# A second timetable for the units that run without row blocks, in a fused attention and state-space kernel

## The chip, the core and the metric

The kernel runs on one core of one Trainium2 chip. The metric is the device time of one execution in microseconds (us), as the median of three runs.

## The reference, cut to what matters

The input has 8 images of 256 channels and 48 x 48 = 2304 positions. Layer 0 is a top-16 attention between the positions of an image, layer 1 two stacked state-space (Mamba) blocks. Both add their result to their input:

```
x = x + L0(groupnorm(x))
    tokens @ W -> feat, pos;  pos /= |pos|;  sim = pos pos^T          (2304 x 2304)
    softmax over the 16 largest of each row, times feat
x = x + L1(groupnorm(x))          two times, d = 0 and 1:
    xn = layernorm(x);  xi, z = split(xn @ in_w);  xc = silu(conv4(xi))
    dt_r, B, C = split(xc @ xp_w);  dt = softplus(dt_r @ dtp_w + b)
    for t:  h = h * exp(dt[t] * A) + dt[t] * B[t] * x[t]              (512 channels x 16 states)
            y[t] = sum over states of h * C[t]
    x = ((y + xc * D) * silu(z)) @ out_w
```

## The kernel before

**Tiles and stages.** Positions are cut into 6 chunks of 384. One chunk of one block (c, d) is a *unit*; an image has 12 units, in an order in which block 1 follows block 0 by two chunks. A unit has 16 *steps* (32 of the 512 channels times 16 states, laid out as 128 partitions x 4 states), and a step has 2 *parts* of 2 states, so a unit is 32 parts and the program 8 x 12 x 32 = 3072 parts. The loop at the end of the kernel runs over the part number m. "Hook h" below is the place of a part within its unit, 0 to 31.

**What a part is.** ScalarE makes the decays exp(dt * A) into one of two PSUM banks (`decay`, L868, two instructions of 385 columns). VectorE runs the recurrence over them (`run_scan`, L883, 770 columns). The product with C is made either by VectorE directly after the scan (L885, 768 columns) or by GpSimd one step later (`pool_part`, L911, one instruction of 768 columns for one part of a step, or of 1536 for both). Who makes it is read from `SHARE`: three patterns of 16 letters, G for GpSimd and V for VectorE, read twice per unit. Pattern 0 is for units 1 to 9 of images that have a successor, pattern 1 for units 0, 10 and 11 of these, pattern 2 for the last image. GpSimd also makes the product dt * x * B, two steps ahead (`make_bx`, L844, 1536 columns a step), and dt * x (`times_x`, L792). TensorE sums over the states (`sum_states`, L929). On VectorE, `gate` (L935) takes that sum.

**The order of the work.** It is written out by hand in two tables, `between` (issued before the scan of a part) and `behind` (after it). A row `(7, copy_z, 0)` says that this function of unit w is issued at part 32 w + 7; places below 0 lie in the unit before, and places above 31 in the one after. Each engine works through its own instructions in this order. Around the change stand: the layer norm (`mean`, `center`, `square`, `variance`, `root`, `root_end`, `spread_root`, `scale`, `normal`; -37 to -22), the projections `in_proj` 0 to 7, `silu_x` (-14) and `softplus` (-10), which change ScalarE's table twice each, `times_x`, which also stores its results for the reload by `load_rep`, and `copy_z` / `silu_z`, which empty the projections 4 to 7 from PSUM. `out_proj` and `leave` of the unit before lie at hooks 6 to 8. The PSUM tiles of all of these, and of layer 0, come from one pool of three ("mm"). SyncE issues all transfers of the loop, in the same order; `load_rep` takes four for a step, into one of three dt buffers in turn.

**Layer 0 runs beside it.** Image 0's layer 0 runs alone at the start. For the other images a generator (`layer0`, stepped once a part by `Ahead.go`) makes one step after each scan: statistics of the input (6 chunks and 8 steps), then projections of the 6 chunks, then 18 row blocks, a new one every 16 parts. A row block has four VectorE instructions over 2304 columns. The generator of image 1 starts at part `EARLY` = -20; each next one starts as soon as its predecessor has ended. The row blocks begin only at a part that is in phase (`PHASE`, a multiple of 16). Before unit 0 of image b issues `load_v` (42 parts ahead of its first scan), `Ahead.finish` runs all steps that image b's generator has left, at once.

**Lines that the steps use.** L180 to L182 are the last three VectorE instructions of the reciprocal root (`rsqrt_end`); L164, L165 its start on ScalarE; L172 to L176 its end on GpSimd for layer 0's norms; L242 the input's statistics; L353, L357, L362 layer 0's copies on ScalarE; L530 the end of a row block; L676 `center`; L706 `scale`; L642 `in_proj`; L742 `taps`; L801 `copy_z`; L806 to L810 `silu_z`; L778 to L787 `softplus`; L960 `leave` of block 0; L616 `load_rep`.

Of the kernel before, what the change touches and what calls it, by code (L numbers as in the profile page):

```python
# [10 lines left out]
AF = mybir.ActivationFunctionType  # L11
# [4 lines left out]
P = 128  # L16
# [9 lines left out]
def tile_conv_preact(  # L26
# [44 lines left out]
    EARLY = -20  # L71


    SHARE = ("GGVGGGVVGGGGGGVG", "GGGVGVVGVVVGVGVG", "VGVGVGVVGGVVGGVG")
# [92 lines left out]
    def rsqrt_end(eng, r, var, eps, name):  # L167
# [11 lines left out]
        nc.scalar.activation(t, r, AF.Square)  # L179
        eng.scalar_tensor_tensor(var, var, eps, t, ALU.add, ALU.mult)  # L180
        eng.tensor_scalar(var, var, -0.5, 1.5, ALU.mult, ALU.add)
        eng.tensor_mul(r, var, r)  # L182
# [51 lines left out]
    def input_stats(b, pool, mm0, ahead, kept):  # L234
# [14 lines left out]
        found = []  # L249
        yield from group_stats(st, found, mm0, f"a{b}")  # L250
        known[b] = found

    def layer0(b, left, pool, ps0, alone):
# [27 lines left out]
        if not alone:  # L281
            if b not in known:
                yield from input_stats(b, pool, mm0, 2, None)
            loaded[0] = load_chunk(pool, x[b], 0, "x", f"xt_{b}_0", 3)
        yield
# [239 lines left out]
        def finish(t):  # L525
# [14 lines left out]
            (21, weights, 3), (4, top, 3), (14, turn, 0), (15, weights, 0), (6, others, 3),  # L540
            (-5, similar, 4), (-8, keep_similar, 0), (-5, keep_similar, 2), (24, turn_back), (18, weigh, 1),
            (17, weigh, 0), (1, top, 1), (-9, similar, 0), (-8, similar, 1), (-7, similar, 2),
            (22, average), (-6, similar, 3), (-7, keep_similar, 1), (-3, keep_similar, 3), (0, top, 0),
            (-3, keep_similar, 4), (15, turn, 1), (10, others, 4), (5, others, 0), (3, top, 2),
            (6, add_top), (11, invert), (5, others, 2), (17, turn, 2), (20, turn, 3),
            (15, weights, 1), (18, turn, 4), (18, weights, 2), (21, weigh, 3), (7, others, 1),
            (19, weigh, 2), (20, weights, 4), (21, weigh, 4), (24, finish),
# [126 lines left out]
    def center(unit):  # L674
        v = unit["v"]
        nc.vector.tensor_tensor(  # L676
            v, v, unit["lm"].unsqueeze(1).to_broadcast([P, CB, T]), ALU.subtract
        )
# [153 lines left out]
    def on_pool(unit, i, p):  # L832

        stage = 2 if unit["b"] + 1 == B else 0 if TOPK[0] <= unit["at"] < TOPK[1] else 1
        return SHARE[stage][(i * PARTS + p) % BLOCK] == "G"

# [115 lines left out]
    def leave(unit, cb):  # L952
# [18 lines left out]
        (-15, taps, 1), (38, out_proj, 0), (-15, taps, 2), (-14, taps, 3), (-34, square),  # L971
        (39, leave, 0), (23, load_rep, "dt", 14), (5, load_rep, "dt", 5), (-4, load_bc, 1), (38, out_proj, 1),
        (17, load_d, 2), (-17, tap, 1), (18, load_rep, "dtx", 13), (-8, times_x, 1), (19, gate, 1),
        (-22, normal), (1, load_rep, "dt", 3), (0, load_rep, "dtx", 4), (15, load_rep, "dt", 10), (6, load_rep, "dtx", 7),
        (10, load_rep, "dtx", 9), (12, load_rep, "dtx", 10), (20, load_rep, "dtx", 14), (11, gate, 0), (-29, spread_root),
        (-19, load_in, 5), (33, load_out), (-22, load_in, 0), (21, load_rep, "dt", 13), (-20, tap, 0),
        (-10, step_size, 1), (9, copy_z, 2), (-18, in_proj, 2), (2, load_rep, "dtx", 5), (10, sum_states, 0),
        (13, load_rep, "dt", 9), (29, gate, 2), (9, silu_z), (7, load_rep, "dt", 6), (19, load_rep, "dt", 12),
        (-6, load_rep, "dtx", 1), (-14, load_in, 7), (-30, root), (9, load_rep, "dt", 7), (4, load_d, 1),
        (-24, load_in, 3), (17, load_rep, "dt", 11), (14, load_rep, "dtx", 11), (-13, x_proj), (-17, load_in, 6),  # L980
        (-3, load_d, 0), (4, load_rep, "dtx", 6), (-4, load_rep, "dtx", 2), (-42, load_v),
    ]
    behind = [
        (-12, split), (-3, load_rep, "dt", 1), (3, in_proj, 4), (-10, step_size, 0), (-5, load_rep, "dt", 0),
        (-8, load_rep, "dtx", 0), (-15, tap, 3), (-1, load_rep, "dt", 2), (-28, scale), (16, load_rep, "dtx", 12),
        (11, load_rep, "dt", 8), (8, in_proj, 6), (17, sum_states, 1), (-14, silu_x), (25, load_rep, "dt", 15),
        (-37, affine), (1, times_x, 2), (7, copy_z, 0), (8, load_rep, "dtx", 8), (-17, tap, 2),
        (-10, softplus), (-16, in_proj, 3), (3, load_rep, "dt", 4), (-29, load_in, 2), (6, in_proj, 7),
        (35, gate, 3), (-2, load_rep, "dtx", 3), (8, copy_z, 1), (40, leave, 1), (-3, times_x, 3),
        (22, load_rep, "dtx", 15), (-16, load_in, 4), (29, load_d, 3), (-37, mean), (-19, taps, 0),  # L990
        (-19, in_proj, 1), (-10, load_bc, 0), (33, sum_states, 3), (-30, root_end), (-9, times_x, 0),
        (-22, load_in, 1),
    ]
    inner, outer = {}, {}
    for w, unit in enumerate(units):
        for table, rows in ((inner, between), (outer, behind)):
            for part, f, *args in rows:
                table.setdefault(HOOKS * w + part, []).append((f, unit, args))
# [91 lines left out]
```

## Time and profile before

| what | us |
|---|---|
| median of 3 runs (9910.5 to 9914.0) | 9911.15 |
| the profiled execution | 9912.53 |
| its span, first to last instruction | 9910.6 |
| layer 0 of image 0, up to the first scan | 463.0 |
| 12 units of image 0, from the first scan | 1214.5 |
| 12 units of image 2 | 1196.6 |
| 12 units of the last image | 1074.0 |
| VectorE / GpSimd / ScalarE / TensorE busy | 8963.6 / 8970.3 / 7319.0 / 7983.7 |

The profile gives for each engine the busy time and, for each idle stretch, what ended it. No engine is busy over the whole span, so the units are read one by one: the start of every 32nd scan cuts the span into units, and busy time, waits and order of instructions are read in these windows.

### The profile page before, as it was taken

Reading aid. Unit: us, or ns where it says so; the run is one execution under the profiler, and the core shown is the slowest. Engines: PE = TensorE matmul, PEld = TensorE weight load, DVE = VectorE, ACT = ScalarE, POOL = GpSimd, SP = SyncE. Lnnn points to the kernel's source line nnn. Section 1 sums busy time; section 2 is a strip of 40 time slices with the busy share of each in tenths; the row PEclk is TensorE's granted clock in tenths of the full one; section 3 lists DMA queues with packets and bytes.
Section 4 is the critical chain, followed back from the end, with each engine's and each line's share of the span. In section 5 each row is a group of like instructions: output and inputs, shape, how many; then the busy total and the mean of one; then the engine's idle time right before and its main releaser. Section 6 shows DMA issues by size and latency. Waiting matters only on the chain. (4 is left out here: it accounts for less than half of the span.)

```text
span 9910.6 us, 133908 instructions
## 1 busy us (share of the span) xinstructions
PE 7983.7 (81%) x36761; PEld 4396.4 (44%) x36761; DVE 8963.6 (90%) x7993; ACT 7319.0 (74%) x15966; POOL 8970.3 (91%) x3980
## 2 busy tenths in 40 slices
PE   8878887888878887788877888778887888866665
PEld 6634444444434454444444445344444444422222
DVE  5589997999989999899998999899998999988898
ACT  4577876777767777777777787777786777766766
POOL 1199997999989999899998999899998999999999
PEclk9989998899979998899988999889997999977777
DMA  1244444444444445444454444544445444544554
GB/s 35 58 124 131 129 134 131 133 125 136 129 140 128 132 130 145 129 126 134 131 145 126 130 130 133 142 130 123 137 129 147 121 134 126 139 136 132 144 139 122
DMA packets 1241871, 1269.01 MB, mean 128 GB/s; under 512 B 266496, under 2 KB 1214208, under 8 KB 1241120
## 3 DMA queue, kind: packets, MB, share of 16 engines
q1 hardware_dynamic: 1240576, 1260.46, 46.2%
q8 instruction: 293, 4.80, 0.2%
q14 instruction: 458, 3.75, 0.1%
q10 hardware_dynamic: 544, 0.00, 0.0%
HBM read 1046.58 MB, written 212.86 MB: 127 GB/s over the span
## 5 line engine op out<-in xcount | busy, mean ns | idle before, releaser
L844 POOL TENSOR_TENSOR bx<-BC,dtxr 128x1536 f32<-128x1536 f32 x1536 | 5298.3, 3452 | 168.6 <-PE y L929 114.9
L868 ACT ACTIVATE da<-dtr,A_sb 128x385 f32<-128x385 f32 x6144 | 3590.3, 585 | 880.8 <-DVE bx L883 540.0
L883 DVE TENSOR_TENSOR_SCAN bx<-da,bx 128x770 f32<-128x770 f32 x2040 | 3523.5, 1748 | 207.8 <-ACT da L868 166.0
L911 POOL TENSOR_TENSOR bx<-bx,BC 128x1536 f32<-128x1536 f32 (+1 forms) x1320 | 3303.7, 2503 | 246.2 <-DVE bx L883 232.0
L883 DVE TENSOR_TENSOR_SCAN da<-da,bx 128x770 f32<-128x770 f32 x1032 | 1809.9, 1754 | 212.4 <-ACT da L868 156.2
L642 PE MATMUL pe<-vn,inw 128*128 128x384 f32 (+1 forms) x3072 | 1248.8, 539 | 443.2 <-DVE xr L964 88.0
L433 PE MATMUL psim<-pos 128*128 128x512 f32 x2520 | 1225.5, 618 | 192.3 <-ACT sim L442 75.9
L504 PE MATMUL po<-feat,aT 128*128 128x256 f32 x5184 | 1359.6, 412 | 20.0 <-ACT aT L493 14.1
L929 PE MATMUL y<-bx,sel 128*32 128x384 f32 x12288 | 1234.1, 536 | 53.1 <-POOL bx L911 43.8
L504 PEld LDWEIGHTS po<-feat,aT 128*128 128x128 f32 x5184 | 1028.1, 205 | 356.4 <-issue 111.0
L885 DVE TENSOR_TENSOR bx<-da,BC 128x768 f32<-128x768 f32 x1032 | 989.3, 959 | 35.5
L642 PEld LDWEIGHTS pe<-vn,inw 128*128 128x128 f32 x3072 | 586.1, 205 | 950.9 <-issue 186.3
L433 PEld LDWEIGHTS psim<-pos 128*128 128x128 f32 x2520 | 486.6, 208 | 768.2 <-issue 414.0
L929 PEld LDWEIGHTS y<-bx,sel 128*32 128x32 f32 x12288 | 396.6, 119 | 879.2 <-issue 731.4
L742 DVE SCALAR_TENSOR_TENSOR xc<-pe,cw,xc 128x384 f32<-128x384 f32 x1152 | 696.6, 612 | 36.5 <-ACT xc L734 9.4
L772 PE MATMUL pd<-dbl,dtp_sb 16*128 16x384 f32 x768 | 437.1, 686 | 322.6 <-ACT dt L781 174.9
L899 ACT COPY h_st<-da 128x2 f32<-128x2 f32 x832 | 132.0, 159 | 687.7 <-DVE bx L885 681.1
L493 ACT ACTIVATE aT<-pt 128x512 f32<-128x512 f32 (+1 forms) x720 | 388.3, 548 | 244.3 <-PE pt L485 239.0
L484 PE MATMUL pt<-ident,sim 128*128 128x128 f32 x2592 | 536.2, 290 | 32.1 <-DVE v L706 16.0
L947 PE MATMUL pw<-z,ow 128*128 128x384 f32 x1536 | 525.1, 495 | 20.1 <-ACT h_st L899 7.3
L476 ACT ACTIVATE rest<-left,three 128x512 bf16<-128x512 f32 (+1 forms) x720 | 465.5, 670 | 52.3 <-DVE left L461 52.3
L485 PE MATMUL pt<-minus,rest 128*128 128x128 bf16 x2592 | 489.5, 224 | 5.9 <-ACT rest L476 5.8
(156 smaller groups left out, 9998.9 us busy)
## 6 DMA issues: line engine op xcount, KB each, us to landing
dtxr<-dtx_d SPq DMA_DIRECT2D x6144, 48.0 KB, 1.9
dtr<-dt_d SPq DMA_DIRECT2D x6144, 48.0 KB, 1.9
BC<-bc_d SPq DMA_DIRECT2D x768, 192.0 KB, 3.9
inw<-in_in_wT_dram SPq DMA_DIRECT2D x768, 128.0 KB, 2.3
dtx_d<-dtx SPq DMA_DIRECT2D x384, 192.0 KB, 2.1
dt_d<-dt SPq DMA_DIRECT2D x384, 192.0 KB, 2.3
ow<-in_out_wT_dram SPq DMA_DIRECT2D x96, 512.0 KB, 4.1
dmat<-diag SPq DMA_DIRECT2D x384, 64.0 KB, 2.3
```

The costliest lines, as they stand in the source:

```text
L433: nc.tensor.matmul(pm, pos[:, k, t * P : (t + 1) * P], pos[:, k, c0 : c0 + w], start=(k == 0), stop=(k == CB - 1),)
L484: nc.tensor.transpose(pt[:, q], row["sim"][:, r], ident)
L504: nc.tensor.matmul(row["po"], aT[:, m % PT, :], feat[:, m, :], start=(m == 0), stop=(m == NB - 1))
L642: nc.tensor.matmul(pe, w[:, k], unit["vn"][:, k, lo:], start=(k == 0), stop=(k == CB - 1))
L742: nc.vector.scalar_tensor_tensor(unit["xc"][e], unit["pe"][e][:, k : k + T], cw[:, unit["d"], e, k : k + 1], unit["xc"][e], ALU.mult, ALU.add,
L844: nc.gpsimd.tensor_tensor(bx[:, :, 1:], unit["BC"][0], unit["dtxr"][i].unsqueeze(1).to_broadcast([P, Q, T]), ALU.mult,)
L868: nc.scalar.activation(da[:, s * (1 + T) : (s + 1) * (1 + T)], unit["dtr"][i], AF.Exp, scale=A_sb[:, unit["d"], i, p * HQ + s : p * HQ + s ...
L883: nc.vector.tensor_tensor_scan(h, da, g, 0.0, ALU.mult, ALU.add)
L885: nc.vector.tensor_tensor(bx[:, :, 0:T], da.rearrange("p (q t) -> p q t", q=HQ)[:, :, 1:], unit["BC"][1][:, qs], ALU.mult,)
L911: nc.gpsimd.tensor_tensor(g[:, :, 0:T], g[:, :, 1:], unit["BC"][1][:, qs], ALU.mult)
L929: nc.tensor.matmul(y[j * G : (j + 1) * G, :], sel, unit["bx"][k * J + j][:, q, 0:T], start=False, stop=True, skip_group_check=True,)
L947: nc.tensor.matmul(pw, unit["ow"][:, k, cb * P : (cb + 1) * P], unit["z"][k], start=(k == 0), stop=(k == DB - 1),)
```

## The change

It has six parts.

1. `EARLY` becomes -24.
2. For images whose statistics are not known yet (2 to 7), `layer0` requests the first chunk before the group statistics and not after them, and has one step less.
3. `SHARE` has 32 letters a unit. Pattern 0 keeps 24 G and 8 V; patterns 1 and 2 go from 16 G to 17 G.
4. The Newton step on VectorE has two instructions in place of three: ScalarE's square is scaled by 1/2, and the result is negative. `center` therefore takes the mean minus the value.
5. In the timetable of the units beside row blocks, eight rows move.
6. A second pair of tables, `between_spare` and `behind_spare`, is used for all places outside units 1 to 9, and for the whole last image. 25 rows stand elsewhere than before, among them `copy_z` 0, `in_proj` 4 and 5, `taps` 0 and 1, `spread_root`, `scale`, `gate` 3, `times_x` 2 and 3, `load_bc` 0. In these tables `normal` (-22) is issued ahead of `scale` (-21), so it takes the value before that multiplication; and dt rows 14 are requested (20) into the buffer of rows 11 before the two decays of step 11 (issued at hooks 21 and 22), which then read rows 14. What these units compute differs in those two places.

```diff
-    EARLY = -20
-    SHARE = ("GGVGGGVVGGGGGGVG", "GGGVGVVGVVVGVGVG", "VGVGVGVVGGVVGGVG")
+    EARLY = -24
+    SHARE = (
+        "GGVGGGVVGGGGGGVGGGVVGGGVGGGGGGVG",
+        "GGGGVGVVGVVVGVGVGGGGVGVGGVVVGVGV",
+        "VGVGVGVGVGVGGGVGGGVVVGVVGGVVGGVG",
+    )
...
-        nc.scalar.activation(t, r, AF.Square)
+        nc.scalar.activation(t, r, AF.Square, scale=0.5 ** 0.5)
         eng.scalar_tensor_tensor(var, var, eps, t, ALU.add, ALU.mult)
-        eng.tensor_scalar(var, var, -0.5, 1.5, ALU.mult, ALU.add)
-        eng.tensor_mul(r, var, r)
+        eng.scalar_tensor_tensor(r, var, 1.5, r, ALU.subtract, ALU.mult)
...
+        if then is not None:
+            then()
         yield from group_stats(st, found, mm0, f"a{b}")
...
-            if b not in known:
-                yield from input_stats(b, pool, mm0, 2, None)
-            loaded[0] = load_chunk(pool, x[b], 0, "x", f"xt_{b}_0", 3)
-        yield
+            if b in known:
+                first_chunk()
+                yield
+            else:
+                yield from input_stats(b, pool, mm0, 2, None, first_chunk)
...
-            v, v, unit["lm"].unsqueeze(1).to_broadcast([P, CB, T]), ALU.subtract
+            v, unit["lm"].unsqueeze(1).to_broadcast([P, CB, T]), v, ALU.subtract
...
-        return SHARE[stage][(i * PARTS + p) % BLOCK] == "G"
+        return SHARE[stage][i * PARTS + p] == "G"
...
+    place = {(f, *args): part for part, f, *args in between + behind}
+
+    def beside_none(m):
+        image, part = divmod(m, HOOKS * len(order))
+        return image + 1 == B or not TOPK[0] * HOOKS <= part < TOPK[1] * HOOKS
```

Places that the text speaks of ("out" is behind the scan, "in" before it):

| row | before | beside row blocks | spare |
|---|---|---|---|
| load_rep dt 0 | -5 out | -3 out, after dt 1 | -5 out |
| times_x 3 | -3 out | 0 in | -8 out |
| load_in 4 | -16 out | -8 out | -16 out |
| load_rep dtx 8, 10, 14 | 8 out, 12 in, 20 in | 8 in, 10 out, 21 in | 9 in, 12 in, 20 in |
| load_rep dt 14 | 23 in | 23 in | 20 in |
| out_proj 0 | 38 in | 37 in | 38 in |
| copy_z 0 | 7 out | 7 out | 6 out |
| in_proj 4, 5 | 3 out, 7 in | the same | 4 out, 7 out |
| taps 1 | -15 in | -15 in | -15 out |
| spread_root, scale | -29 in, -28 out | the same | -22 in, -21 out |
| normal | -22 in | -22 in | -22 in |
| load_bc 0 | -10 out | -10 out | -12 out |
| mean, center | -37 out, -35 in | the same | -38 out, -34 in |
| gate 3 | 35 out | 35 out | 37 in |

## The prediction

> **What bounds the kernel now.** I read the page's busy times first. VectorE and GpSimd are both near nine tenths, so neither number alone says what a change is worth. Then I cut the span at every 32nd scan and asked for busy times by unit. Columns: start:end, length, then busy us of TensorE matmul, weight load, VectorE, ScalarE, GpSimd, then clock and DMA.
>
> ```profile
> PE 7983.7 (81%) x36761; PEld 4396.4 (44%) x36761; DVE 8963.6 (90%) x7993; ACT 7319.0 (74%) x15966; POOL 8970.3 (91%) x3980
> ...
> 1450.50:1570.50 120.00, 81.54 (x388) 45.99 (x386) 100.06 (x104) 75.20 (x173) 90.04 (x46) 0.81 0.48 135
> 2666.40:2768.70 102.30, 67.53 (x302) 33.74 (x300) 89.28 (x94) 67.73 (x157) 89.94 (x46) 0.77 0.56 157
> ...
> 4766.90:4863.80 96.90, 85.35 (x411) 48.11 (x410) 94.41 (x84) 77.66 (x173) 96.30 (x35) 0.94 0.47 129
> 5161.30:5268.40 107.10, 83.99 (x352) 46.25 (x351) 83.82 (x74) 76.73 (x161) 89.78 (x62) 0.85 0.48 134
> ...
> 8926.00:9015.60 89.60, 54.71 (x224) 24.35 (x223) 80.20 (x70) 63.33 (x145) 83.65 (x32) 0.77 0.49 136
> ```
>
> These are unit 10 of image 0, the same of image 1, unit 7 and unit 11 of image 3, and unit 1 of the last image. Beside row blocks (63 units, 95.6 to 101.7, mean 98.5) GpSimd is busy 96.3: nearly full. Units 10, 11 and 0 (21 units: medians 101.5, 107.2, 103.8) have less work and take longer; there it is waits. The last image (89.3) lies in between. So four places, four limits. The waits of each come next (engine, line, releaser: total, times, longest).
>
> ```profile
> DVE xr L530 <- PE pr L521: 11.2, 1, 11.2
> ...
> DVE da L883 <- ACT da L868: 9.4, 4, 6.9
> DVE z L935 <- PE y L929: 7.5, 3, 4.0
> DVE st L242 <- DMA xs<-in_x_dram: 6.2, 1, 6.2
> ...
> DVE da L883 <- ACT da L868: 31.2, 15, 3.2
> DVE bx L883 <- ACT da L868: 28.7, 16, 3.1
> ...
> L883 DVE TENSOR_TENSOR_SCAN bx<-da,bx 128x770 f32<-128x770 f32 x2040 | 3523.5, 1748 | 207.8 <-ACT da L868 166.0 <-POOL bx L856 32.8 <-POOL dtx L792 0.8
> ```
>
> The first row is unit 10 of image 0, the next three units 10 and 11 of image 3, then two of nine units of the last image. The last is the costliest group of scans over the whole run (count, busy, mean ns, then idle before them and by whom): 166.0 us until decays were there, 32.8 until GpSimd was. VectorE hardly waits for GpSimd: it waits for ScalarE's decays, behind table changes, and for TensorE.
>
> **A. Image 1's row blocks (EARLY).** Counting steps from the code: image 1's generator starts at -20, has its projections done at part 29, and the phase lets it begin only at 44. At 342 `finish` runs the 17 steps left at once: hook 21 of that unit lasts 16.1 us, of which VectorE waits 11.2 as shown. Starting at -24 it is done at 25 and begins at 28, as all later images do; one step is left at 342. Image 0 then costs what image 2 does: 1214.5 - 1196.6 = 17.9. Four steps move ahead of the first scan (two loads, two matmul groups of about 1.1); cost 0 to 4, taken 1. Sum -17, between -19 and -12.
>
> **B. The 63 units beside row blocks.** Pattern 0 moves one VectorE product from hook 22 to hook 19. At hook 20 VectorE waits 0.55 for decays (the mean), which the product then fills; at hook 22 it leaves 0.87 (start to start). The softplus burst behind hook 22 has its decays ready at 4744.1 in unit 6 of image 3, and the scan there starts at 4745.3, so it can come 0.9 earlier. The Newton step loses one instruction, 0.2 start to start (0.169 each in the rows). Together 1.07 less on VectorE. GpSimd has the same work, but of its 2.2 idle 1.5 are waits for a scan; that is all it can give back. Against it: dt 0 is requested two hooks later, behind dt 1. In that unit dt 1 is requested at 4760.2, 1.8 per four requests, so dt 0's last piece leaves at about 4763.4 and lands 1.9 later, 4765.3; its decay now starts at 4764.65, and the scan at 4767.0. Late by 0.7, of which 0.2 reaches the scan if it comes no earlier, more if it does. Behind this wait on ScalarE stand all decays. I take 1.0 - 0.4 = 0.6 a unit: 63 x 0.6 = -38. Bounds: 63 x 1.07 = -67, and +20 if the lateness eats it all and 0.3 more. `times_x` 3 moving to hook 0, its two stores past dt 0 and three requests of `load_rep`, `load_in` 4, dtx 8, 10, 14 and `out_proj` 0 move within stretches in which neither VectorE nor GpSimd waits above 0.1 a unit for a transfer; 0, and some tenths if that cover is gone.
>
> **C. Units 10, 11 and 0 of seven images.** VectorE loses one product (0.96) and one Newton instruction (0.2): 21 x 1.16 = -24. `copy_z` 0 one part earlier frees a PSUM tile. What that is worth shows in the last image: `in_proj` 7 (second row) stands 3.39 for a tile and runs when `leave` gives one; then ScalarE's second `copy_z` waits 1.74 for its matmul, and the scan 2.02.
>
> ```profile
> 8944.99 0.47 ACT L960 COPY vo<-pw 128x384 f32<-128x384 f32 x1
> 8945.52 5.60 PE L642 MATMUL pe<-vn,inw 128*128 128x384 f32 x12 [3.39 <-ACT vo L960]
> 8949.86 0.48 ACT L801 COPY z<-pe 128x384 f32<-128x384 f32 x1 [1.74 <-PE pe L642]
> 8951.55 1.77 DVE L883 TENSOR_TENSOR_SCAN da<-da,bx 128x770 f32<-128x770 f32 x1 [2.02 <-ACT da L868]
> ```
>
> In units 10, 11 and 0 the same place costs VectorE 4.0, 3.6 and 1.5 (gate for the sum); in unit 10 TensorE is then full of row-block matmuls, so not all of it goes. 0 to 2.7 each, taken 1.4: 20 x 1.4 = -28. One step less (part 2) moves layer 0's projections by one part: the start of the norm's root, two copies and a square (0.30 + 0.20 + 0.56 + 0.84 = 1.9) now come before and not behind the softplus of unit 11, where the scan waits 6.88 and GpSimd 4.17. ScalarE has 1.82 idle just ahead. 6 x 1.9 = -11, between 0 and -16; shifted elsewhere it may hit `silu_x`, up to +6. The first chunk's earlier request takes away ScalarE's 3.56 for it, but VectorE waits for GpSimd there (2.06): nothing. That wait is also where the added G costs: 1.685 a unit by the row of 768 columns, charged once per image, 7 x 1.7 = +12. `load_bc` 0 now stands directly behind the store that it reads (1.5 to land), ahead of the statistics' chunk: the 6.2 wait keeps or grows by 1.2; taken 0. Sum -51, between -100 and +10.
>
> Here a rule speaks against the change. The Trainium skill (GPSIMD Engine Reference, Engine selection) gives two-input elementwise work to VectorE because GpSimd is about twice as slow. By the rows it is 1.685 to 0.959, 1.76 times. By twice, the added products would cost 1.92, 33 x 0.23 = 8 more on GpSimd; still within its idle 11.8 to 18.4 a unit. So the move pays where VectorE is the later one, as here. For the bursts that stay, the same notes (ScalarE: Activation LUTs, What ACT_TABLE_LOAD costs) give 2.66 per change with a drain of 1.38. In the trace a load takes 1.283 and the first softplus starts 0.02 behind it. By the rule a burst would be 2.8 longer and the 1.9 would drown; by the row it counts.
>
> **D. The last image.** VectorE: 0.96 + 0.2 + the wait at hook 10 (mean 1.39) = 2.55 of 8.1 idle and 80.5 busy. GpSimd: 84.0 + 1.7 = 85.7, against 89.3 - 2.55 = 86.8; its waits for dt (1.45) and for the sum (0.6) may hold. I take 2.2: 12 x 2.2 = -26, between -36 and 0. `taps` 1 behind the scan moves a burst of 1.85; `spread_root`, `scale`, `gate` 3, mean and center keep their durations: 0. (For `center` the PSUM operand comes first now; `gate` has it first and takes 0.545 for 384 columns, the last addition of `leave` has it second and takes 0.539.)
>
> **The added wait.** In the spare units decays 11 read the buffer that dt 14 fills, requested at hook 20 and wanted at 21. Requests at hook 20 leave about one hook early and need 1.8 + 1.9. 0 to 1 each, taken 0.3: 33 x 0.3 = +10. Decays, scan and gate stand behind it.
>
> Sum: -17 - 38 - 51 - 26 + 10 = -122, from 9912.5 of the profiled execution (span 9910.6 and 1.9 around it). The median stands 1.4 lower: 9911.15 - 122 = 9789.
>
> **Rivals.**
> - *GpSimd is the bound* (0.22). B gives nothing, since 96.3 of 98.5 is full; C gives half (-25), D 1.0 a unit (-12), A stays: -17 - 25 - 12 + 10 = -44, 9867. For it: the busy row; against it: scans hardly wait for GpSimd.
> - *The waits of C dissolve* (0.15). Units 10, 11 and 0 fall to the 98.0 of their neighbours: 6 x (101.5 + 107.2 + 103.8 - 294) = -111 for -51, and B reaches -50: about -194, 9717. Against it: the statistics' wait and the bursts stay.
> - *Slower: dt 0 comes late* (0.05). BC pieces in that queue land up to 4.5 after request. If dt 0 does, decay 0 and all of ScalarE slip 2.6 in each of 63 units, +164 for -38: 164 - 17 - 51 - 26 + 10 = +80, 9991. It decides from 84 / 63 = 1.3 a unit. For it: it is asked behind dt 1 and BC; against it: SyncE is freed of two requests' waits.
> - *It doesn't do what it says* (0.03): the shift makes as many collisions as it removes, and VectorE's saving ends in ScalarE's waits: only A, and B to D cancel with the added wait: about 9900.
>
> **How the numbers follow.** My sum has 0.55. A measurement of this kernel can tell 0.2% (20 us) from no change. Faster: 0.55 + 0.22 + 0.15 = 0.92; same 0.03; slower 0.05. The range reaches from near the third case to the first rival with its spread: 9700 to 9878.
>
> **What would show it.** A: hook 21 of unit 10, image 0, falls from 16.1 to about 2. B: units 4 to 9 near 97.4, GpSimd's wait at hook 28 below 1. C: gate's wait at hook 10 smaller, the 6.88 near 5. D: `in_proj`'s 3.39 gone, units near 87. Wrong if decay 0 waits for dt 0, if the statistics' wait grows beyond 8, or if scans begin to wait for L844.

## The result, and the profile after

The changed kernel takes 9813.64 us (median of 4 runs, 9801.14 to 9814.34); the kernel before, measured again beside it, takes 9912.25. The ratio is 0.9898, with an interval of 0.988 to 0.9915. That is 99 us less; 122 were predicted. The profiled execution took 9813.77, its span 9812.0, which is 98.6 below the span before. The experiments are compared by the same two measures: the difference of the medians taken on the same chip, and the unit times of the profiled execution. The unit times come from one execution of each kernel. Some of their differences are scatter: `e1_early` and `e8_newton` change next to nothing in most units 11 and 0, yet the means of these units differ by up to about 1 between them and the kernel before. The first scan lies anywhere between 459.5 and 467.2. A single difference of that size says nothing.

The page's busy times come first, then two of its costliest groups (count, busy, mean ns, then idle before them and by whom).

```profile
span 9812.0 us, 133959 instructions
...
PE 7958.7 (81%) x36761; PEld 4336.7 (44%) x36761; DVE 8904.6 (91%) x7864; ACT 7304.4 (74%) x15938; POOL 9023.9 (92%) x3971
...
L892 DVE TENSOR_TENSOR_SCAN bx<-da,bx 128x770 f32<-128x770 f32 x2073 | 3578.1, 1747 | 263.6 <-ACT da L877 232.4
L920 POOL TENSOR_TENSOR bx<-bx,BC 128x1536 f32<-128x1536 f32 (+1 forms) x1311 | 3353.6, 2558 | 70.5 <-DVE bx L892 66.0
```

VectorE lost 59 us of work and GpSimd gained 54. The group of scans shown has those whose product GpSimd makes; it now waits 232.4 for decays, against 166.0 before. The other group has those whose product VectorE makes, before and after:

```profile
L883 DVE TENSOR_TENSOR_SCAN da<-da,bx 128x770 f32<-128x770 f32 x1032 | 1809.9, 1754 | 212.4 <-ACT da L868 156.2 <-POOL bx L856 20.5 <-POOL bx L844 15.8
```

```profile
L892 DVE TENSOR_TENSOR_SCAN da<-da,bx 128x770 f32<-128x770 f32 x999 | 1752.0, 1754 | 123.7 <-ACT da L877 81.2 <-POOL bx L865 15.6 <-ACT h_st L930 11.2
```

Together the scans wait 314 for decays where they waited 322. So VectorE has less work, but it waits for ScalarE almost as long as before. In two kernels that come below, `e10_four` and `e11_old_rows`, the same sum is 260 and 258. The scan is L892 now, the gate L944, the decay L877, GpSimd's product L920; `times_x` L801 and L804, `load_rep` L625, `in_proj` L651.

These are the units of the prediction's first block (columns as there): unit 10 of image 0, then unit 7, 10 and 11 of image 3, unit 0 of image 4, unit 1 of the last image.

```profile
1444.30:1547.80 103.50, 70.00 (x306) 34.50 (x304) 88.02 (x90) 67.16 (x154) 94.04 (x47) 0.76 0.58 159
4712.50:4810.80 98.30, 87.23 (x413) 48.43 (x412) 94.36 (x83) 77.80 (x175) 96.78 (x35) 0.93 0.48 130
5007.20:5113.50 106.30, 70.92 (x310) 35.63 (x312) 88.22 (x91) 67.27 (x155) 93.78 (x47) 0.76 0.55 157
5113.50:5214.60 101.10, 80.61 (x359) 44.80 (x360) 81.90 (x73) 78.64 (x162) 89.23 (x59) 0.91 0.52 141
5214.60:5311.00 96.40, 74.05 (x318) 37.76 (x318) 83.82 (x75) 70.62 (x152) 85.44 (x61) 0.84 0.46 123
8844.60:8931.00 86.40, 55.26 (x222) 23.54 (x222) 78.84 (x69) 63.16 (x144) 86.28 (x35) 0.80 0.52 141
```

Unit 10 of image 0 fell from 120.0 to 103.5, unit 11 of image 3 from 107.1 to 101.1. The unit beside row blocks, unit 7 of image 3, did not fall (96.9 to 98.3), and an ordinary unit 10 grew: 106.3, where 101.6 was the median of images 1 to 5. VectorE's waits in unit 10 and in unit 11 of image 3 and in nine units of the last image (total, times, longest):

```profile
DVE st L245 <- DMA xs<-in_x_dram: 7.3, 2, 5.9
DVE z L944 <- PE y L938: 4.8, 2, 4.2
DVE xr L973 <- PE pw L956: 2.4, 1, 2.4
DVE bx L892 <- ACT da L877: 2.2, 1, 2.2
DVE da L892 <- ACT da L877: 1.3, 1, 1.3
...
DVE bx L892 <- ACT da L877: 7.4, 2, 6.6
...
DVE bx L892 <- ACT da L877: 34.4, 23, 3.1
DVE z L944 <- PE y L938: 13.8, 7, 3.0
```

The burst's 11.2 is gone, but `gate` in unit 10 still waits 4.2 for the sum, and three waits (the third to fifth row) have joined it. In unit 11 the long wait for decays is 6.6 where it was 6.9. Both would have been clearly smaller had the prediction's part C been right in its parts.

Mean unit times of the profiled executions. "Beside" are units 1 to 9 of images 0 to 6 (63 units); 10, 11 and 0 are these units of images 0 to 6; 12 are of the last image.

| kernel | beside | unit 10 | unit 11 | unit 0 | last image | span |
|---|---|---|---|---|---|---|
| before | 98.26 | 103.27 | 104.62 | 103.98 | 89.50 | 9910.6 |
| after | 97.97 | 104.99 | 100.91 | 97.35 | 87.99 | 9812.0 |
| e1_early | 98.30 | 100.77 | 103.54 | 103.28 | 89.49 | 9884.9 |
| e2_chunk | 98.24 | 103.88 | 100.55 | 103.93 | 89.32 | 9881.7 |
| e3_share | 97.39 | 104.89 | 103.82 | 102.19 | 89.12 | 9843.9 |
| e4_copyz | 98.29 | 103.21 | 103.11 | 104.60 | 88.69 | 9895.2 |
| e8_newton | 98.20 | 103.60 | 104.23 | 104.11 | 89.49 | 9906.7 |
| e5_dt0 | 97.82 | 105.50 | 101.88 | 97.03 | 87.87 | 9808.9 |
| e6_u10 | 97.83 | 105.89 | 100.53 | 97.00 | 88.03 | 9810.5 |
| e9_dt14 | 97.93 | 104.02 | 98.10 | 98.95 | 89.49 | 9814.7 |
| e7_order | 97.87 | 103.56 | 98.09 | 101.25 | 89.36 | 9822.8 |
| e11_old_rows | 97.38 | 106.59 | 100.59 | 97.44 | 88.04 | 9784.5 |
| e10_four | 97.41 | 101.55 | 98.42 | 101.06 | 87.75 | 9759.6 |
| e12_mix | 97.41 | 103.63 | 97.99 | 101.26 | 87.76 | 9770.0 |

The account of the whole change, from the first two rows: first scan 1.9 earlier (within its scatter); beside row blocks 63 x -0.29 = -18.2; unit 10 of image 0 -16.4, of the six other images +4.7 each = +28.4; unit 11 -25.9; unit 0 -46.4; last image -18.2. Sum -98.6.

### The profile page after: what moved, and what is told of

Same layout as the page of the kernel before. It is cut to its first block, busy times and chain, and to the rows that moved or that the text cites. A ratio compares the mean times of both kernels' runs of the same rounds, so it can differ in the third digit from the quotient of the medians.

```text
span 9812.0 us, 133959 instructions
## 1 busy us (share of the span) xinstructions
PE 7958.7 (81%) x36761; PEld 4336.7 (44%) x36761; DVE 8904.6 (91%) x7864; ACT 7304.4 (74%) x15938; POOL 9023.9 (92%) x3971
## 4 chain that ended last, share of the span: by engine, by line
DVE 33%; ACT 24%; DMA 11%; PE 11%; SPq 10%; issue 7%; POOL 4%; ACTq 0%; DVEq 0%; POOLq 0%
DVE bx L892 11%; ACT da L877 10%; SPq L625 8%; DVE da L892 8%; DVE xc L751 5%; DMA dtr<-dt_d 4%; DVE bx L894 3%; DMA BC<-bc_d 3%; DVE top L464 2%; DVE left L467 2%; POOL bx L920 2%; PE po L514 2%; POOL bx L853 2%; DMA dtxr<-dtx_d 2%; ACT rest L486 1%
## 5 line engine op out<-in xcount | busy, mean ns | idle before, releaser
L877 ACT ACTIVATE da<-dtr,A_sb 128x385 f32<-128x385 f32 x6144 | 3588.1, 584 | 868.6 <-DVE bx L892 375.1
L892 DVE TENSOR_TENSOR_SCAN bx<-da,bx 128x770 f32<-128x770 f32 x2073 | 3578.1, 1747 | 263.6 <-ACT da L877 232.4
L920 POOL TENSOR_TENSOR bx<-bx,BC 128x1536 f32<-128x1536 f32 (+1 forms) x1311 | 3353.6, 2558 | 70.5 <-DVE bx L892 66.0
L892 DVE TENSOR_TENSOR_SCAN da<-da,bx 128x770 f32<-128x770 f32 x999 | 1752.0, 1754 | 123.7 <-ACT da L877 81.2
L651 PE MATMUL pe<-vn,inw 128*128 128x384 f32 (+1 forms) x3072 | 1214.7, 526 | 329.6 <-issue 50.9
L938 PE MATMUL y<-bx,sel 128*32 128x384 f32 x12288 | 1266.0, 536 | 109.9 <-POOL bx L920 103.1
L514 PEld LDWEIGHTS po<-feat,aT 128*128 128x128 f32 x5184 | 1022.4, 203 | 343.1 <-issue 107.2
L894 DVE TENSOR_TENSOR bx<-da,BC 128x768 f32<-128x768 f32 x999 | 957.2, 958 | 34.4
L651 PEld LDWEIGHTS pe<-vn,inw 128*128 128x128 f32 x3072 | 566.9, 199 | 845.8 <-issue 206.2
L956 PE MATMUL pw<-z,ow 128*128 128x384 f32 x1536 | 557.0, 509 | 112.8 <-ACT aT L503 52.4
L935 PE MATMUL y<-xc,dmat 128*128 128x384 f32 x768 | 398.3, 606 | 171.7 <-ACT h_st L930 58.5
```

The lines of the kernel that those rows point to most:

```text
L514: nc.tensor.matmul(row["po"], aT[:, m % PT, :], feat[:, m, :], start=(m == 0), stop=(m == NB - 1))
L651: nc.tensor.matmul(pe, w[:, k], unit["vn"][:, k, lo:], start=(k == 0), stop=(k == CB - 1))
L877: nc.scalar.activation(da[:, s * (1 + T) : (s + 1) * (1 + T)], unit["dtr"][i], AF.Exp, scale=A_sb[:, unit["d"], i, p * HQ + s : p * HQ + s ...
L892: nc.vector.tensor_tensor_scan(h, da, g, 0.0, ALU.mult, ALU.add)
L894: nc.vector.tensor_tensor(bx[:, :, 0:T], da.rearrange("p (q t) -> p q t", q=HQ)[:, :, 1:], unit["BC"][1][:, qs], ALU.mult,)
L920: nc.gpsimd.tensor_tensor(g[:, :, 0:T], g[:, :, 1:], unit["BC"][1][:, qs], ALU.mult)
```

## The experiments

My theory was the prediction's list: each part is worth its own term, and two terms cost (dt 0 late, the wait for dt 14). The rivals were that the second timetable brings the gain of units 10, 11 and 0, and that some other moved row eats what the patterns give. First each part by itself, on the kernel before; then parts undone in the changed one; then the parts that gained, put together.

The list of the change leaves out one row. In the row blocks' own timetable, `others` 3 (ScalarE makes 512 columns, 0.71) goes from part 6 of a block to part 7. The changed kernel and all kernels made from it have it at 7, the kernel before and all made from that at 6, and no run moves it alone. Beside row blocks it leaves no mark: `e11_old_rows` and `e12_mix` with it at 7 stand at 97.38 and 97.41, `e3_share` and `e10_four` with it at 6 at 97.39 and 97.41. Its last instance in image 3 lies at hook 29 of unit 9.

**Image 1's generator earlier.** `e1_early`:

```diff
-    EARLY = -20
+    EARLY = -24
```

> The kernel before with EARLY = -24 alone. Theory (step A): image 1's row blocks begin at part 28 and leave one step for the forced finish, so hook 21 of unit 10 of image 0 falls from 16.1 to about 2 and image 0 from 1214.5 to about 1197; time 9912 - 17 = 9895. Rival: the 17 forced steps cost what they cost anywhere, and come back as longer units 1 to 9 of image 0; time 9905 to 9912. The span up to the first scan should stay at 463 within 4 either way.

9890.72 against 9912.72, ratio 0.998 (0.9973 to 0.9987): -22. Unit 10 of image 0 fell from 120.0 to 102.3 and image 0 from 1214.5 to 1190.8 (1197 was worked out); the first scan came 2.0 later, which is within its scatter. Hook 21 of that unit lasts 2.7 here and 1.7 in the changed kernel, where it lasted 16.1. A stands as it was worked out; the rival, that the forced steps come back elsewhere, falls.

**The chunk ahead of the statistics.** `e2_chunk` is part 2 of the change, on the kernel before:

```diff
-            if b not in known:
-                yield from input_stats(b, pool, mm0, 2, None)
-            loaded[0] = load_chunk(pool, x[b], 0, "x", f"xt_{b}_0", 3)
-        yield
+            if b in known:
+                first_chunk()
+                yield
+            else:
+                yield from input_stats(b, pool, mm0, 2, None, first_chunk)
```

> The kernel before with the first chunk requested ahead of the group statistics, and so one step less, alone. In the changed kernel units 11 and 0 are 5 and 6.6 shorter, unit 10 is 4.7 longer. Theory 1: the shift by one part makes the gain of units 11 and 0 (fewer collisions of layer 0's ScalarE work with the table changes): units 11 and 0 fall by 3 or more each here, unit 10 stays; time 9912 - 6 x 8 = about 9865. Theory 2: the spare tables make it; here only the root's start in unit 11 (-1.9) counts: 6 x 1.9 = 11, time about 9900. GpSimd's 4.17 at hook 23 of unit 11 goes in either.

9881.75, ratio 0.9971 (0.9964 to 0.9977): -31, nearly three times the 11 of the prediction. Nearly all of it is unit 11: 4.1 at the mean of the seven, and 4.9 at the mean of the six beside which such a generator runs (107.2 to 102.3); units 0 and 10 keep their time within 0.7. GpSimd's wait of 4.2 for the root is gone there; in unit 11 of image 3 the scan's longest wait for ScalarE is 6.0 where it was 6.9. So unit 11 is as theory 1 has it and unit 0 as theory 2 has it, and the time lies between theirs.

**The patterns.** `e3_share` has the three patterns of 32 letters and nothing else:

```diff
-    SHARE = ("GGVGGGVVGGGGGGVG", "GGGVGVVGVVVGVGVG", "VGVGVGVVGGVVGGVG")
+    SHARE = (
+        "GGVGGGVVGGGGGGVGGGVVGGGVGGGGGGVG",
+        "GGGGVGVVGVVVGVGVGGGGVGVGGVVVGVGV",
+        "VGVGVGVGVGVGGGVGGGVVVGVVGGVVGGVG",
+    )
```

> The kernel before with the three new patterns of 32 letters alone. Theory (VectorE is the later one): units 1 to 9 lose 0.3 to 0.6 each, GpSimd's wait at hook 28 falls from 1.3 to below 0.3, the last image loses about 1.0 a unit, units 10, 11 and 0 about 1: -20 - 12 - 20 = time about 9860. Rival (GpSimd is the bound): units 1 to 9 move by less than 0.1, the last image does not gain from the added G and units 10, 11, 0 get longer by up to 1.7: time 9910 to 9945.

9845.18, ratio 0.994 (0.9925 to 0.9955): -67, of which 63 x 0.87 = 55 beside row blocks. This refutes the rival that GpSimd is the bound there. GpSimd's waits in units 1 to 9 of image 3, before and with the patterns:

```profile
POOL bx L911 <- DVE bx L883: 12.7, 15, 1.7
```

```profile
POOL bx L915 <- DVE bx L887: 1.4, 4, 0.5
```

It had 18.3 idle in these nine units (864.7 busy of 883.0), 12.7 of it waiting for a scan. 11.3 of that wait went, because VectorE's product now lies where VectorE waited (hook 20, 0.55 a unit, now 0). Part came back as other waits: 10.5 idle are left (866.0 busy of 876.5), and the nine units are 6.5 shorter.

**The copy one part earlier.** `e4_copyz`, in all units:

```diff
-        (-37, affine), (1, times_x, 2), (7, copy_z, 0), (8, load_rep, "dtx", 8), (-17, tap, 2),
+        (-37, affine), (1, times_x, 2), (6, copy_z, 0), (8, load_rep, "dtx", 8), (-17, tap, 2),
```

> The kernel before with copy_z 0 at 6 instead of 7 alone, in all units. Theory: the TensorE wait of 3.39 ahead of in_proj 7 shortens, the scan's wait for decays at hook 10 of the last image (mean 1.39) goes, units of the last image lose 1.4 (-17), units 10, 11 and 0 up to 1.4 (-28), the others nothing: time about 9870. Rival: the wait only changes its name (gate waits for the sum at hook 10, as the changed kernel's last image shows with 1.54): the last image moves by less than 0.3 a unit, time 9905 to 9912.

9901.22, ratio 0.9991 (0.9983 to 1.0): -11, at the edge of what can be told from nothing. The last image gains 0.81 a unit, between the theory's 1.4 and the rival's 0.3; units 10, 11 and 0 change by -0.06, -1.5 and +0.6, the others by 0. ScalarE's wait of the second copy, in nine units of the last image, before and in this kernel:

```profile
ACT z L801 <- PE pe L642: 13.1, 11, 2.9
```

```profile
ACT z L801 <- PE pe L642: 3.5, 9, 0.9
```

The mechanism is that of the prediction. In units 10, 11 and 0 it was carried over from the last image by likeness, and there it gives nothing that can be told from scatter.

**The shorter Newton step**, with `center` turned, `e8_newton`:

```diff
-        eng.tensor_scalar(var, var, -0.5, 1.5, ALU.mult, ALU.add)
-        eng.tensor_mul(r, var, r)
+        eng.scalar_tensor_tensor(r, var, 1.5, r, ALU.subtract, ALU.mult)
```

> The kernel before with the shorter Newton step and the turned center alone. Theory: 0.2 of VectorE's time a unit where VectorE is the later engine, and no other price for the operand order: 96 x 0.1 to 0.2 = 10 to 19 shorter, time 9893 to 9903. Rival: the saved instruction ends in the next wait for decays: within 5 of 9912. center should keep 0.947 within 0.01.

9909.34 against 9910.07, ratio 0.9995 (0.9987 to 1.0004). No difference that this measurement can tell, and a gain of more than 13 is excluded; 98.20 for 98.26 beside row blocks. `center` keeps its duration (0.945 after).

**dt 0 asked at its old place** in the changed kernel, `e5_dt0`. Here and in `e6_u10` and `e11_old_rows` the spare units keep the two places where the change computes something else; in `e9_dt14` the scaling alone does.

```diff
-        (-12, split), (-3, load_rep, "dt", 1), (3, in_proj, 4), (-10, step_size, 0), (-3, load_rep, "dt", 0),
+        (-12, split), (-3, load_rep, "dt", 1), (3, in_proj, 4), (-10, step_size, 0), (-5, load_rep, "dt", 0),
```

> The changed kernel with load_rep dt 0 back at -5 beside row blocks. Units 1 to 9 gained 0.87 each from the patterns alone and only 0.29 in the whole change. Theory: dt 0 behind dt 1 at -3 holds decay 0 and takes most of the difference, as the new waits of scans for decays at hooks 0 (0.48) and 6 (0.41) say: they go here, units 1 to 9 fall from 97.97 to about 97.4, time 9813 - 63 x 0.55 = about 9778. Rival: other rows of that table (times_x 3 at hook 0, load_in 4) make it: less than 0.15 a unit, time above 9803.

9808.19, ratio 0.9895 (0.988 to 0.991). Against the changed kernel's 0.9898 that is no difference; the unit times show 0.15 a unit beside row blocks (97.97 to 97.82), where the theory had 0.55. ScalarE's waits for dt in units 1 to 9 of image 3, in the changed kernel and in this one:

```profile
ACT da L877 <- DMA dtr<-dt_d: 29.5, 16, 3.7
```

```profile
ACT da L877 <- DMA dtr<-dt_d: 11.8, 7, 3.0
```

Sorted by place, over all 63 units, decay 0 (issued at hook 31) waits 1.94 a unit in the changed kernel and 0 here. So dt 0 does come late. But 11.8 remain, nearly all for decays at hook 5 (0.95 a unit over the 63). That is step 3, whose request nobody moved.

**Unit 10 on the other timetable.** `e6_u10`:

```diff
-        return image + 1 == B or not TOPK[0] * HOOKS <= part < TOPK[1] * HOOKS
+        return image + 1 == B or not TOPK[0] * HOOKS <= part < (TOPK[1] + 1) * HOOKS
```

> The changed kernel with the spare tables for units 0 and 11 and the last image only, unit 10 by the table beside row blocks. Unit 10 grew by 4.7 in the whole change and by nothing like it in the parts alone. Theory: the spare rows in unit 10 make it, where the last row blocks still fill TensorE until hook 12 (the addition of leave waits 1.67 for its matmuls at hook 6): unit 10 falls by 3 to 4.5, time 9813 - 7 x 3.5 = about 9790. Rival: the change of tables itself costs, and moves to unit 11, which grows by as much: within 5 of 9813.

9808.48, ratio 0.9896 (0.9881 to 0.9911). Unit 10 stays where it was: 107.2 as the median of images 1 to 5, against 106.2. The theory falls, and the rival's shift into unit 11 did not come either. So it isn't the spare table by itself that lengthens unit 10; with either of the new tables it is long, with the rows of before it is not (102.7 in `e10_four`).

The traces show what goes with it. In the changed kernel ScalarE's decays wait 2.8 for dt in the mean unit 10, nearly all at hooks 3 and 5; in all kernels with a new table there it is 2.5 to 4.6, and in the kernel before, `e3_share` and `e10_four` at most 0.1. Against `e10_four`, a unit 10 of the changed kernel is 3.44 longer, and hooks 5 and 6 together are 3.41 longer; the other hooks cancel. Step 3's decays in unit 10 of image 3, changed kernel and `e10_four`:

```profile
5019.10 1.20 ACT L877 ACTIVATE da<-dtr,A_sb 128x385 f32<-128x385 f32 x2 [1.49 <-DMA dtr<-dt_d]
```

```profile
4990.32 1.21 ACT L879 ACTIVATE da<-dtr,A_sb 128x385 f32<-128x385 f32 x2 [0.23 <-DMA dtr<-dt_d]
```

SyncE's queue at the start of that unit of the changed kernel, whose first scan is at 5007.2:

```profile
5008.04 0.34 SPq L804 DMA_DIRECT2D dtx_d<-dtx  x1
5008.43 0.42 SPq L804 DMA_DIRECT2D dt_d<-dt  x1
5008.94 1.79 SPq L625 DMA_DIRECT2D dtr<-dt_d  x4
```

The spare table has `times_x` 2 at hook -1, ahead of the request of dt 2, and the old one behind the request of dt 3. SyncE stands from 5006.61 until GpSimd's product, begun at 5007.01, is done, and dt 2 and dt 3 are requested 1.7 and 6.5 behind the first scan (0.8 and 5.8 in `e10_four`). In `e6_u10` it is `times_x` 3 at hook 0 that stands ahead of dt 3. No run moves these rows alone in unit 10, so this is read from the traces and not measured apart. Nor is it all: the waits do not put the kernels in the order of their unit 10 (`e12_mix` waits 3.6 at 103.63, the changed kernel 2.8 at 104.99).

**dt 14 back to hook 23** in the spare units, `e9_dt14`; and with it `spread_root` and `scale` back to their old places ahead of `normal`, `e7_order`:

```diff
-        (-15, taps, 2), (-14, taps, 3), (-35, square), (39, leave, 0), (20, load_rep, "dt", 14),
+        (-15, taps, 2), (-14, taps, 3), (-35, square), (39, leave, 0), (23, load_rep, "dt", 14),
```

```diff
-        (11, gate, 0), (-1, times_x, 2), (-22, spread_root), (-19, load_in, 5), (33, load_out),
+        (11, gate, 0), (-1, times_x, 2), (-29, spread_root), (-19, load_in, 5), (33, load_out),
...
-        (-8, times_x, 3), (-8, load_rep, "dtx", 0), (-15, tap, 3), (-1, load_rep, "dt", 2), (-21, scale),
+        (-8, times_x, 3), (-8, load_rep, "dtx", 0), (-15, tap, 3), (-1, load_rep, "dt", 2), (-28, scale),
```

> The changed kernel with dt 14 back at 23 in the spare tables, nothing else (normal still takes the value ahead of scale; the decays of step 11 read their own rows). With all three rows back, units 0 grew by 3.9 and the last image by 1.4 a unit, units 11 fell by 2.8. Theory: scale and spread_root made that (out_proj waits for the tile that scale frees), so here units 0 and the last image stay within 0.5: time 9808 to 9820. Rival: the later dt request makes it (SyncE then stands at hook 23 ahead of the stores of times_x): the last image grows by 1 or more a unit, time 9825 to 9845.

> The changed kernel with three spare rows back at the places before: spread_root -29, scale -28 (so normal again takes the scaled value) and dt 14 at 23 (so the decays of step 11 read their own rows). Units 0 lost 6.6 in the whole change and at most 1.8 in any part alone. Theory: the time does not hang on these rows; units 0, 11 and the last image stay within 0.5 each: time 9805 to 9825. Rival: the gain of unit 0 comes from taking the multiplication and its spread off hooks 3 and 4, where layer 0's projections and the out projection queue for the same three PSUM tiles: unit 0 grows by 3 to 6 again and the last image by 0.5 each: time 9840 to 9865.

`e9_dt14`: 9811.91, ratio 0.9896 (0.9878 to 0.9913), as the changed kernel within the interval. That hides movements in both directions. Unit 11 falls by 2.8 and unit 10 by 1.0; the last image rises by 1.5 a unit and unit 0 by 1.6. So the rival is right in the last image, though the time is the theory's. GpSimd's waits in nine units of the last image, changed kernel and `e9_dt14`:

```profile
POOL dtx L801 <- ACT dt L790: 9.4, 8, 1.5
POOL bx L920 <- DVE bx L892: 4.5, 5, 1.6
...
POOL dtx L801 <- DMA dtx_d<-dtx: 0.7, 1, 0.7
```

```profile
POOL dtx L801 <- DMA dtx_d<-dtx: 12.7, 8, 3.1
POOL dtx L801 <- ACT dt L790: 11.5, 9, 1.5
POOL bx L920 <- DVE bx L892: 4.5, 6, 1.6
```

With dt 14 asked at 23, GpSimd's next `times_x` waits 1.4 a unit for the store of an earlier one. In `e9_dt14` the requests of dt 14 stand ahead of that store, here in unit 3 of the last image:

```profile
9077.87 2.18 SPq L625 DMA_DIRECT2D dtr<-dt_d  x4
9080.15 0.37 SPq L804 DMA_DIRECT2D dtx_d<-dtx  x1
...
9082.25 1.00 POOL L801 TENSOR_TENSOR dtx<-dt,xc 128x384 f32<-128x384 f32 x1 [1.59 <-DMA dtx_d<-dtx]
```

GpSimd has little slack in these units (770.7 busy of 786.3 in the changed kernel), so this counts nearly in full: the nine units are 13.3 longer. But the wait is of the spare table's own making. That table has three `times_x` within two hooks (-9, -8, -8), the old one only two. In `e12_mix` the last image runs by the old table with dt 14 at 23: the wait is 0 there, and the unit takes 87.76. `e7_order`: 9824.95, ratio 0.991 (0.9895 to 0.9925); its span is 8 longer than that of `e9_dt14`, and unit 0 rises by another 2.3. Its theory, that units 0, 11 and the last image stay within 0.5, falls in all three. Of the 6.6 that unit 0 gained, about 2.3 came with the scaling behind `normal` and 1.6 with the early dt 14: 3.9 with the two places where the change computes something else.

**The eight rows beside row blocks put back.** `e11_old_rows` has `between` and `behind` as before the change, the rest as changed (only the eight rows are written out):

```diff
     between
-    (37, out_proj, 0), (0, times_x, 3), (8, load_rep, "dtx", 8), (21, load_rep, "dtx", 14),
+    (38, out_proj, 0), (12, load_rep, "dtx", 10), (20, load_rep, "dtx", 14),
     behind
-    (-3, load_rep, "dt", 0), (10, load_rep, "dtx", 10), (-8, load_in, 4), (-20, load_in, 1),
+    (-5, load_rep, "dt", 0), (8, load_rep, "dtx", 8), (-3, times_x, 3), (-16, load_in, 4), (-22, load_in, 1),
```

> The changed kernel with the rows beside row blocks all as before the change (the spare tables stay). Units 1 to 9 were 97.4 with the patterns alone and are 98.0 in the whole change; dt 0 back alone made 97.8. Theory: the eight moved rows together cost that: units 1 to 9 at 97.4, time 9813 - 63 x 0.55 = about 9778. Rival: the shorter Newton step or the state in which unit 0 hands over makes it: units 1 to 9 stay above 97.8, time above 9800.

9782.64 against 9917.75, ratio 0.9864 (0.9849 to 0.9879), as the theory has it, and a span 27.5 shorter than the changed kernel's. Beside row blocks a unit takes 97.38, as with the patterns alone (97.39). So the eight rows cost 0.59 a unit, 63 x 0.59 = 37, of which unit 10 gives some back. Nine units of image 3, changed kernel, this one, and the patterns alone (columns as in the blocks of units):

```profile
4123.10:5007.20 884.10, 766.72 (x3619) 422.97 (x3621) 850.27 (x740) 692.52 (x1520) 867.66 (x325) 0.93 0.49 131
```

```profile
4112.70:4990.40 877.70, 765.25 (x3610) 425.97 (x3609) 849.51 (x741) 693.95 (x1519) 866.31 (x323) 0.93 0.49 132
```

```profile
4143.20:5019.70 876.50, 760.85 (x3609) 425.89 (x3608) 850.69 (x750) 695.30 (x1519) 865.96 (x323) 0.93 0.48 132
```

All three have the same work on VectorE within 1.2 and on GpSimd within 1.7. The 6.4 between the first two are almost all waits. Which row makes them can be read from SyncE's queue at the start of unit 7 of image 3, whose first scan is at 4712.5 (changed kernel; start, duration, what is requested):

```profile
4714.04 1.76 SPq L625 DMA_DIRECT2D dtxr<-dtx_d  x4
4718.17 0.34 SPq L804 DMA_DIRECT2D dtx_d<-dtx  x1
4718.55 0.43 SPq L804 DMA_DIRECT2D dt_d<-dt  x1
4719.09 0.38 SPq L949 DMA_DIRECT2D ow<-in_out_wT_dram  x1
4719.57 1.90 SPq L625 DMA_DIRECT2D dtr<-dt_d  x4
```

and in the kernel before, first scan at 4767.0:

```profile
4767.73 1.75 SPq L616 DMA_DIRECT2D dtxr<-dtx_d  x4
4769.58 0.40 SPq L940 DMA_DIRECT2D ow<-in_out_wT_dram  x1
4770.08 1.84 SPq L616 DMA_DIRECT2D dtr<-dt_d  x4
4773.85 0.34 SPq L795 DMA_DIRECT2D dtx_d<-dtx  x1
```

`times_x` 3 now stands at hook 0, so its store (L804) lies ahead of the four requests of dt 3. Between 4715.8 and 4718.17 SyncE issues nothing: it waits for GpSimd's product, which runs at 4717.15 behind the product with C. dt 3 is requested 7.1 behind the first scan, where it was 3.1. Its decays then wait for it, as the decays of dt 0 do at hook 31:

```profile
4711.18 1.21 ACT L877 ACTIVATE da<-dtr,A_sb 128x385 f32<-128x385 f32 x2 [1.28 <-DMA dtr<-dt_d]
4725.95 1.21 ACT L877 ACTIVATE da<-dtr,A_sb 128x385 f32<-128x385 f32 x2 [1.59 <-DMA dtr<-dt_d]
```

The wait at hook 5 is 1.20 a unit in the changed kernel, 0.95 with dt 0 back, and 0 in this one and in the kernel before. `times_x` 3 was not put back alone, so its share of the 0.43 a unit that dt 0 leaves is read from the trace and not measured apart.

**The four parts that gained, without the second timetable.** `e10_four` is the kernel before with `EARLY`, the chunk, the patterns and `copy_z` 0 at 6:

```diff
-    EARLY = -20
+    EARLY = -24
-    SHARE = ("GGVGGGVVGGGGGGVG", "GGGVGVVGVVVGVGVG", "VGVGVGVVGGVVGGVG")
+    SHARE = (
+        "GGVGGGVVGGGGGGVGGGVVGGGVGGGGGGVG",
...
+                yield from input_stats(b, pool, mm0, 2, None, first_chunk)
...
-        (-37, affine), (1, times_x, 2), (7, copy_z, 0), (8, load_rep, "dtx", 8), (-17, tap, 2),
+        (-37, affine), (1, times_x, 2), (6, copy_z, 0), (8, load_rep, "dtx", 8), (-17, tap, 2),
```

> The kernel before with four parts: EARLY -24, the chunk ahead of the statistics, the new patterns, copy_z 0 at 6; one timetable, whose other rows are those of before, and the old Newton step. Alone these gave -22, -31, -67 and -11. Theory 1: they add up, and the second timetable and the moved rows beside row blocks are worth nothing or less: 9912 - 131 = 9781, range 9770 to 9800. Theory 2: they overlap (the patterns and the chunk remove the same waits), and the second timetable makes up the rest: 9815 or more. Units 1 to 9 are 97.4 by theory 1.

9768.17 against 9917.75, ratio 0.9849 (0.9834 to 0.9864): -150 (interval 135 to 165), and a span 52 below the changed kernel's. Alone the four gave -22, -31, -67 and -11, together about -132; the parts add, and a surplus over that is not clear of noise. In the unit table they gain more together than alone in the last image (1.75 against 0.01 + 0.18 + 0.38 + 0.81 = 1.38) and in units 10 and 0, and less in unit 11 (6.2 against 7.5). Its busy times, nine units of image 3, and unit 1 of the last image:

```profile
PE 7906.1 (81%) x36761; PEld 4348.6 (45%) x36761; DVE 8915.9 (91%) x7960; ACT 7317.8 (75%) x15938; POOL 9019.4 (92%) x3971
```

```profile
4101.80:4979.00 877.20, 759.24 (x3609) 425.40 (x3608) 850.75 (x749) 695.18 (x1519) 864.38 (x323) 0.93 0.49 132
8794.20:8881.00 86.80, 56.76 (x223) 24.54 (x224) 79.00 (x70) 63.26 (x144) 85.14 (x33) 0.76 0.52 140
```

It is faster than the changed kernel although VectorE is busier by 11. Unit 0 is worse without the spare table (101.06 against 97.35), units 10 and 11 are better (101.55 and 98.42 against 104.99 and 100.91).

**Both together.** `e12_mix` is `e11_old_rows` with `copy_z` 0 at 6, and the spare table only in units 0, 10 and 11, with dt 14 at 23 and `spread_root` and `scale` at their old places:

```diff
-        return image + 1 == B or not TOPK[0] * HOOKS <= part < TOPK[1] * HOOKS
+        return image + 1 < B and not TOPK[0] * HOOKS <= part < TOPK[1] * HOOKS
```

> The changed kernel with the rows beside row blocks as before but copy_z 0 at 6, the spare tables in units 0, 10 and 11 only and there with spread_root, scale and dt 14 at their places before (so nothing of the computation is changed), the last image by the table beside row blocks. From the parts: units 1 to 9 at 97.4, units 10, 11, 0 at 103.6, 98.1, 101.3 (as with the three rows back), the last image at 88.5: time about 9783. If the second timetable is worth something without the two misplaced rows, this is at least 10 shorter than the kernel of four parts; else it is not.

9768.29, ratio 0.985 (0.9835 to 0.9864), the same as `e10_four`. So where dt 14 and the scaling stand as before, the spare table brings nothing in units 0, 10 and 11 (302.9 for the three, 301.0 in `e10_four`). What unit 0 gained by it, it gained by the two places where the change computes something else.

## Why the prediction was right in its sum, and where its steps failed

The measured 9813.64 is 25 above the predicted 9789 and well within 9700 to 9878. That the sum is so near is in part luck. Its terms A to D come to -132, the added wait to +10. The four parts that gain give 150 by themselves (`e10_four`), and all the rest of the change takes 51 back. So the gains were put a little too small, and what the moved rows cost much too small. Step by step:

- **A, -17: right.** -16.4 in unit 10 of image 0 (-18.3 with the first scan), -22 alone.
- **B, -38: -18.2. The step that failed is its last sentence**, which put `times_x` 3 at hook 0, its two stores and the other moved rows at nothing. The cover it named (no engine waits above 0.1 a unit for a transfer) described the kernel before. The stores wait for GpSimd, and dt 3 stands behind them. The eight rows cost 0.59 a unit, 37 in all (`e11_old_rows`). The first half of B was good: 1.07 was expected of the pattern and the Newton step, 0.87 came, all of it by the pattern. The term for dt 0 had the right mechanism (late by 1.94 at the mean, 0.7 worked out), and its removal gave only 0.15. The wait for dt 3 that then remains (0.95 a unit) is the likely reason; it was not removed alone.
- **C, -51: -43.9, right only in the sum, by luck.** The copy was sized 1.4 in each of 20 units and is worth 0.3 at the mean; the shift by one part was sized 1.9 in six units 11 and is worth 4.9 in them; unit 10 grew by 4.7, and unit 0 fell by 6.6. The new places of `times_x` 2 and 3 in the spare table are in no term; the waits for dt in unit 10 point to them. Of what was to show it, the 6.88 became 6.64 and the gate's wait in unit 10 went from 3.98 to 4.18. Neither is a confirmation. The statistics' wait at hook 23 went from 6.28 to 6.96 at the mean of images 1 to 5, below the 8 that would have refuted; in image 1 it is 8.1.
- **D, -26: -18.2, too large by 0.7 a unit, and not by the path that was worked out.** The mechanism itself is there. The nine units' waits of `in_proj` for `leave` fell from 19.9 to 8.1, and GpSimd's work rose to 85.6, for which 85.7 was worked out. But of VectorE's wait at hook 10, counted as gone, 1.54 came back as `gate` waiting for TensorE's sum, and GpSimd now has 1.73 idle a unit where it had 5.57: the rival's limit, true in this stage alone. The parts that D counts give 1.75 a unit with the old table (`e10_four`). With the spare table and dt 14 at 23 nothing of it is left (89.49 against 89.50 before), and the early dt 14 then brings 1.5 back.
- **The added wait, +10: wrong in sign for the last image and unit 0.** The trace has no wait of these decays for a transfer at hooks 17 to 24 in any spare unit. The early request of dt 14 shortens the last image by 1.5 a unit, because the stores, issued from hook 23 on, then stand behind fewer requests, and unit 0 by 1.6. It lengthens unit 10 by 1.0 and unit 11 by 2.8, nearly all of that at hook 29; why is open. In the sum nothing is left.
- **The rivals.** "GpSimd is the bound" falls by `e3_share` beside row blocks. "The waits of C dissolve" holds for unit 0 alone. "dt 0 late" was real and small. That the change does not do what it says holds for the second timetable: with it and the eight rows 99 are gained, without them 150.
- **Readings that were off, without effect on a step.** The 63 units beside row blocks have a mean of 98.26 and begin at 90.7 (98.5 and 95.6 were said), the medians of units 10 and 11 are 101.6 and 106.9 (101.5 and 107.2), and the last image has 89.5 a unit (89.3).

Open stay whether the late dt rows are all that lengthens unit 10 by 4.7, and how the 0.43 a unit divides between `times_x` 3 and the six other rows.

## What to carry to other kernels

A queue that one engine works through in order is a schedule of its own. For each row that is moved, look up what the row's own store waits for, and which requests then stand behind that wait; busy engines and the transfer waits of the old profile don't show it. A change of several parts is best taken apart by stage: here four small parts give 150 us, and the rest, the two large ones above all, takes about 50 of it back.

## What the runs showed that I had not expected

- One VectorE instruction less in a chain of small dependent ones gave nothing that can be measured (0.9995, 0.9987 to 1.0004), though 0.2 a unit stood in the sum. One C product moved by three hooks gave 0.87 a unit beside row blocks.
- Moving one generator step by one part was worth 4.9 us in each of six units 11: 1.9 of work on ScalarE had stood behind a softplus, and GpSimd had waited 4.2 for its first piece.
- Between two requests SyncE issued nothing for 2.4 us at the start of a unit while it waited for a product of 0.98, and the four transfers behind it landed 11.2 to 13.3 us behind the first scan, where they had landed 6.8 to 7.4 behind it.
